# The attention layer's run-time loop, moved from ahead of the last tile to behind the last put-off tile

## The chip, the cores and the metric

The kernel runs on one core of a Trainium2 chip. The metric is the device time of one execution in microseconds (us). The time given is the median of three runs. The profile is that of one further execution, taken by the hardware profiler. The engines are called PE (TensorE), DVE (VectorE), ACT (ScalarE), POOL (GpSimd) and SP (SyncE, which issues most of the transfers).

## The reference, cut to what matters

Four graph layers work on 4096 nodes with 256 features and a 0/1 adjacency matrix. Each layer's result is added to its input and normalized. Layer 1 does two steps of attention with nucleus sparsification, and layer 2 multiplies its neighbour sums by a weight:

```python
# layer 1, for n in range(2):
probs = softmax((Xa @ W1.T @ W2.T) @ (Xa @ W3.T).T)
# of each row keep the largest entries whose sum first reaches 0.9, divide by the kept sum
A  = kept(probs, 0.9)
Xf = R @ Xf                  # R: adjacency plus identity, rows divided by their sums
Xa = A @ Xa
Z  = Z + Xf @ U1[n].T + Xa @ U2[n].T
...
# layer 2: neighbours, then the weight (here taken as adj @ (x @ w2[256:512]) + x @ w2[:256])
support = concatenate((x, adj @ x, nef)) @ weight + bias
```

## The kernel before, in words

The 4096 rows are cut into NT = 32 tiles of 128 rows (P = 128). Layer 0 runs first, then the two steps of layer 1 (`run_step`, n = 0 and 1, called steps 0 and 1), then layers 2 and 3.

**A step of layer 1.** One iteration of the loop over i (L954) works on three tiles at once: it makes the logits of tile i + 2, finds the threshold of tile i + 1, and multiplies tile i. The function `pieces` (L695) writes out the order on PE by hand in NLC = 8 groups g. In step 1 it transposes the kept rows `e` of tile i (`turn`, L716, copied by ACT at L719) and multiplies them with `xa` (L741). The list `ops` says which other functions are called after which group. When a tile is multiplied, `after` (L810) gives two functions that are called in the groups 1 and 2 of the next iteration: `s1` (`mix`: transposes at L177, products with U1 and U2 at L794, the sum on DVE at L796) and `s2` (two layernorms with DVE lines L185 to L196, L819, L820 and the power on POOL at L191; then `put`, which writes the rows into `x2_d` in DRAM). Before tile i is mixed, `fetch` (L767) loads three 128 KB pieces on SP (L777).

**Finding the threshold.** DVE takes 64 candidates of each row (`tops`, L498 and L502), sums them (`pick`) and, in `settle`, sets what is below the threshold to zero: one pass at L628 and four passes over a quarter of the row each at L633. A row for which 64 candidates do not decide is "bad". `flag` (L552) counts the bad rows of a tile on PE (L562, L563) and writes their numbers into a list in DRAM with an indirect DMA (L576). `later["base"]` holds how many there are so far.

**Put-off tiles.** The bad rows are gathered from the list into extra tiles of 128 rows. Step 1 has four of them that are always done (`LATER = (1, 4)`, `put_off`, L869). They are called put-off tiles 0 to 3 here; their buffers and lines in the profile end in `_l`. Each is a generator that is advanced a stage at a time between the groups of `pieces`; `finish` (L936) runs the stages that are left and multiplies the tile. For put-off tiles DVE needs five passes over the whole row (L468) to find the threshold, then L482, L403 and the lines above. Their rows go back with indirect DMAs on POOL (`put`, L762), since they lie anywhere.

**The run-time loop.** If there are more bad rows than four tiles hold, `left_over` (L896) does the rest: two DVE instructions make the trip count (L899, L900), each engine loads it into a register (L901), and a loop (L902) runs over tiles of 128 rows, with a bit-by-bit search in place of the candidates. In the profile it makes no trip: its body has no record. In step 1 it stands at the head of the iteration i = 31, after tile 30's `s1` and `s2` and before tile 31 is multiplied. Its body uses the buffer `es[0]`, the keys `kS` and `xa`.

**Tile 31.** It is multiplied after the loop. So that it does not overwrite what the loop wrote for its own bad rows, `flag` makes a list of targets for tile 31 alone, `to_last` (L575), in which a bad row points to a spare row behind the 4096. `put` then writes tile 31 with an indirect DMA on POOL over `x2_d` (L762). Layer 0 writes tile 31 of `x2_d` once, so that all of it has been written.

**Products with layer 2's weight.** After the last tile, `z_room` (L828) loads the weight into `es[1]`, and 32 calls of `zu_tile` load a tile of `x2_d` (L852, four slots), multiply it (L177, L843), copy the result (L846) and write it to `zu_d` (L853). Sixteen stand beside the products of put-off tile 2, sixteen beside the stages of put-off tile 3. A put-off tile that ends after `z_room` makes its own products: in `s2` (L823) it calls `zu` and writes `zu_d` with an indirect DMA (L762).

**Layer 2** begins with four pieces of the adjacency matrix (L1077, 128 KB each, on SP; cast by ACT at L1079), the loads of `zu_d` into a scratch area (L157) which DVE and ACT split into two halves (L142, L143, L144), and four weights on ACT's queue (L84, L131). Its tiles lie where `kS`, `es` and the other buffers of layer 1 were, and each waits until those under it are free. Then PE multiplies (L167).

**Order.** Tile, the framework, puts the instructions in order when the kernel is compiled: for each engine it takes what is ready by its own estimate of the times, with the order of the program as the priority. Waits between engines are semaphores, set for the region of a buffer that an instruction touches; an indirect write counts as a write to the whole of the tensor it names. A run-time loop is one unit in this order. What depends on nothing in it can be put ahead of it.

Of the kernel before, what the change touches and what calls it, by code (L numbers as in the profile page):

```python
# [48 lines left out]
def gnn_stack(ctx, tc, x, adjt, adjn, w0, b0, w1, w2t, w3t, u1t, u2t, ln_g, ln_b, w2, b2, w3, b3, out):  # L49
# [3 lines left out]
    nc = tc.nc  # L53
    N = x.shape[0]
    NT = N // P
# [22 lines left out]
    def half(bank):  # L78
        turns[bank] ^= 1
        return (mm_bank if bank == "mm" else acc_bank)[:, turns[bank], :]  # L80
# [25 lines left out]
    x2_d = dram.tile([N + P, D], F32, name="x2_d")  # L106
# [16 lines left out]
    def rows(t, it):  # L123
        return t[it * P : (it + 1) * P, :]
# [46 lines left out]
    def transposed(*srcs):  # L171

        n = 2 * len(srcs)
        ps = ps_tr.tile([P, 4, P], F32, tag="tr", name="tr")
        for s, src in enumerate(srcs):
            for c in range(2):
                nc.tensor.transpose(ps[:, 2 * s + c, :], src[:, c * P : (c + 1) * P], ident)  # L177
        t = work.tile([P, 4, P], F32, tag="xt", name="xt")
        nc.scalar.copy(t[:, :n, :], ps[:, :n, :])  # L179
        return t  # L180
# [33 lines left out]
    with tc.tile_pool(name="l0", bufs=1) as l0, tc.tile_pool(name="l0w", bufs=2) as l0w:  # L214
# [18 lines left out]
        x1 = xpool.tile([P, NT, D], F32, tag="X", name="x1")  # L233
# [53 lines left out]
        def l0_end(it, agg):  # L287
            xi = l0w.tile([P, D], F32, tag="x0i", name="x0i")
            nc.scalar.dma_start(xi, rows(x, it))
            xt = transposed(xi, agg)  # L290
            ps = half("mm")
            for c in range(4):
                nc.tensor.matmul(ps, xt[:, c, :], w0_sb[:, c, :], start=(c == 0), stop=(c == 3))
            t = l0w.tile([P, D], F32, tag="t", name="t")
            nc.vector.tensor_add(t, ps, b0_sb)
            nc.vector.scalar_tensor_tensor(t, t, 0.0, xi, op0=ALU.max, op1=ALU.add)
            ln_apply(x1[:, it, :], t, ln_stats(t))

            x1b = l0w.tile([P, D], F32, tag="x1b", name="x1b")
            nc.vector.tensor_add(x1b, x1[:, it, :], lb_sb)  # L300
            nc.sync.dma_start(rows(x1_d, it), x1[:, it, :])
            nc.sync.dma_start(rows(x1b_d, it), x1b)
            if it == NT - 1:

                nc.sync.dma_start(rows(x2_d, it), x1[:, it, :])

        def l0_keys(it):
            make_keys(transposed(x1[:, it, :]), kS[:, it * P : (it + 1) * P])
# [16 lines left out]
    with tc.tile_pool(name="l1", bufs=1, reuse_waits="tile") as l1:  # L325

        cur = {"late": False, "n": 0, "nef_done": False}
# [224 lines left out]
        def flag(st):  # L552


            pb = half("mm")
            later = st.get("later")
            if later is None:
                nc.tensor.matmul(pb[:1, 0:1], st["bad"], ones_col, start=True, stop=True)
                st["nb"] = small("nbad", 1, I32)[:1, :]
                nc.scalar.copy(st["nb"], pb[:1, :1])  # L560
                return
            nc.tensor.matmul(pb[:, 0:1], ones_sq, st["bad"], start=True, stop=True)  # L562
            nc.tensor.matmul(pb[:, 1:2], before, st["bad"], start=True, stop=True)  # L563
            sofar, slot = small("sofar"), small("slot")
            nc.vector.tensor_add(sofar, later["base"], pb[:, 0:1])

            i = st["tile"]
            at, rows_i = slots_of[cur["n"]][:, i : i + 1], ids[:, i : i + 1]
            nc.vector.scalar_tensor_tensor(slot, pb[:, 1:2], later["base"], spare, op0=ALU.add, op1=ALU.subtract)
            nc.vector.scalar_tensor_tensor(at, slot, st["bad"], spare, op0=ALU.mult, op1=ALU.add)  # L570
            later["base"] = sofar
            if i == NT - 1:

                st["to"] = to = small("to_last", 1, I32, 1)
                nc.vector.scalar_tensor_tensor(to, st["bad"], float(P), rows_i, op0=ALU.mult, op1=ALU.add)  # L575
            nc.gpsimd.indirect_dma_start(  # L576
                out=list_d[cur["n"]], out_offset=bass.IndirectOffsetOnAxis(ap=at, axis=0), in_=rows_i, in_offset=None)
# [318 lines left out]
        def left_over(n, e, later):  # L896

            count = work.tile([P, 1], I32, tag="count_l", name="count_l", bufs=1)
            nc.vector.tensor_scalar(count, later["base"], float(P - 1 - LATER[n] * P), 0.0, op0=ALU.add, op1=ALU.max)  # L899
            nc.vector.tensor_scalar(count, count, P.bit_length() - 1, None, op0=ALU.arith_shift_right)  # L900
            v = nc.values_load(count[0:1, 0:1], min_val=0, max_val=NT - LATER[n])  # L901
            with tc.For_i(0, v, 1) as k:  # L902
                cur["late"] = True
                st, xg = take_rows(n, bass.ds(k * P + LATER[n] * P, P), e)
                all_logits(st, query(xg))
                peak(st)
                exp_rows(st)
                st["t"], st["left"], st["base"] = small("t_thr"), small("left"), None
                for _ in settle(st, True):
                    pass  # L910
                pieces(n, st, None, {})
                for f in after(n, st):
                    f()
                cur["late"] = False

        def run_step(n, es):
# [3 lines left out]
            later = {"base": spare0}  # L920
# [33 lines left out]
            for i in range(-2, NT):  # L954
                st = tiles.pop(i, None)
                cd = tiles.get(i + 1)
                nxt = None
                if i + 2 < NT:

                    nxt = {"tile": i + 2, "q": cur["qs"].pop(0), "e": logits_in(es[i % 2]), "later": later, "G": {}}  # L960
                    tiles[i + 2] = nxt
                if i + 1 == NT:
                    for fs in last:
                        for f in fs:
                            f()
                    last = []
                    left_over(n, es[NT % 2], later)
                ops = {}

                def at(g, f, *args):  # L970
                    ops.setdefault(g, []).append(lambda: f(*args))

                for g, fs in zip((1, 2), last):
                    for f in fs:
                        at(g, f)
                if 0 < i + 2 < NT - 1:
                    turned = []
                    g = 1 if n else 6
                    at(g - 1, lambda i, turned: turned.append(transposed(cur["xa"][:, i + 3, :])), i, turned)
                    at(g, lambda turned: cur["qs"].append(query(None, turned[0])), turned)  # L980
                if cd is not None:
                    peak_groups(cd)
                    at(1, exp_rows, cd)
                for job in jobs:
                    at(1, advance, job)
                if cd is not None:
                    rounds = 8 if n else KEPT // 8
                    at(2, tops, cd, rounds)
                    at(2, pick, cd, rounds)
                    at(4, flag, cd)  # L990
                    if n == 0:
                        for k in range(8):
                            at(4 + k // 2, gather, cd, k)
                    else:
                        at(5, lambda cd: [None for _ in settle(cd)], cd)
                for job in jobs:
                    if n and i + 1 == NT:
                        at(4, advance, job)
                    at(6, advance, job)
                if i + 1 == NT and n == 0:  # L1000
                    cur["next"] = load_halves(es[1 - NT % 2], xf_d, nc.sync)
                if i < 0:
                    now = FIRST[n][i + 2]
                else:
                    now = [i + 2] if FIRST[n][1][-1] < i + 2 < NT else []
                pieces(n, st, nxt, ops, now)
                last = [[f] for f in after(n, st)] if st is not None else []
                if i in starts:
                    k = starts[i]
                    if len(jobs) > (i == NT - 2):  # L1010
                        last = finish(jobs.pop(0), last)
                    e = es[NT % 2] if k + 1 == LATER[n] else es[2]
                    jobs.append({"stages": put_off(n, k, e, later)})
                    if i < NT - 2:
                        advance(jobs[-1])
# [22 lines left out]
            for fs in last:  # L1038
                for f in fs:
                    f()  # L1040

        for n in range(STEPS):
            cur["n"] = n
            with tc.tile_pool(name=f"step{n}", bufs=2, reuse_waits="tile") as cur["w"], \
                    tc.tile_pool(name=f"late{n}", bufs=1, reuse_waits="tile") as cur["lw"]:
                es = [cur["w"].tile([P, N + PAD], F32, tag=f"e{k}", name="e", bufs=1) for k in range(2 + n)]
# [152 lines left out]
```

## Time and profile before

| | |
|---|---|
| median of three runs | 3354.87 us (3349.98 to 3359.43) |
| the profiled execution's own time | 3313.77 us |
| its span, first to last instruction | 3312.0 us |
| mean granted PE clock in it | 0.965 |
| PE busy | 3017.6 us (91%) |
| DVE busy | 2393.5 us (72%) |
| ACT busy | 1873.9 us (57%) |
| POOL busy | 782.7 us (24%) |

The profiled execution is 41.1 us shorter than the median of the runs, and 1.8 us of it lie outside the span. Times in the profile count from the start of the span. Step 1 ends with tile 31's work at about 2585 to 2633 us, the two last put-off tiles up to about 2774 us, and layer 2 starts after that. In a row of the timeline the two first numbers are start and length in us; "x8" says that eight instructions were merged; the bracket gives how long the engine stood idle before it and what ended that.

### The profile page before, as it was taken

Reading aid. Unit: us, or ns where it says so; the run is one execution under the profiler, and the core shown is the slowest. Engines: PE = TensorE matmul, PEld = TensorE weight load, DVE = VectorE, ACT = ScalarE, POOL = GpSimd, SP = SyncE. Lnnn points to the kernel's source line nnn. Section 1 sums busy time; section 2 is a strip of 40 time slices with the busy share of each in tenths; the row PEclk is TensorE's granted clock in tenths of the full one; section 3 lists DMA queues with packets and bytes.
Section 4 is the critical chain, followed back from the end, with each engine's and each line's share of the span. In section 5 each row is a group of like instructions: output and inputs, shape, how many; then the busy total and the mean of one; then the engine's idle time right before and its main releaser. Section 6 shows DMA issues by size and latency. Waiting matters only on the chain. (4 is left out here: it accounts for less than half of the span.)

```text
span 3312.0 us, 46373 instructions
## 1 busy us (share of the span) xinstructions
PE 3017.6 (91%) x14600; PEld 2465.7 (74%) x14600; DVE 2393.5 (72%) x7121; ACT 1873.9 (57%) x3162; POOL 782.7 (24%) x916
## 2 busy tenths in 40 slices
PE   6999888999999997879989898989999787999998
PEld 5888667888888885658877777777788545888886
DVE  6888858878777776357988897888799673444444
ACT  3555666777777774455555454545455333666664
POOL 1111146666666665100000001000100001000000
PEclk9999989999999998889999999999999898999999
DMA  9988367787777776140000111011011133333332
GB/s 175 143 134 139 68 105 130 135 138 137 136 137 137 136 137 143 56 134 30 25 23 23 32 38 31 26 32 39 24 38 30 42 131 126 110 109 107 102 108 81
DMA packets 247906, 300.30 MB, mean 91 GB/s; under 512 B 34688, under 2 KB 201536, under 8 KB 247648
## 3 DMA queue, kind: packets, MB, share of 16 engines
q0 software_dynamic: 46624, 105.07, 22.8%
q1 hardware_dynamic: 188800, 180.93, 18.8%
q10 hardware_dynamic: 12224, 11.23, 1.1%
q8 instruction: 118, 1.93, 0.3%
q14 instruction: 140, 1.15, 0.1%
HBM read 331.17 MB, written 66.58 MB: 120 GB/s over the span
## 5 line engine op out<-in xcount | busy, mean ns | idle before, releaser
L656 PE MATMUL acc_r<-xh,adjq 128*128 128x512 f32 x2048 | 617.5, 433 | 22.4 <-ACT adjq L653 17.7
L741 PE MATMUL acc_bank<-xa,at 128*128 128x256 f32 x2304 | 568.8, 388 | 31.0 <-ACT at L719 30.5
L642 POOL DMA_INDIRECT G<-x_d,cols x512 | 499.4, 975 | 302.2 <-PE acc_bank L733 163.0
L167 PE MATMUL acc<-xh,a 128*128 128x512 f32 x2048 | 516.5, 405 | 17.8 <-DVE xh L144 14.0
L741 PEld LDWEIGHTS acc_bank<-xa,at 128*128 128x128 f32 x2304 | 425.3, 194 | 92.1 <-ACT at L719 41.3
L653 ACT CAST adjq<-adj 128x512 fp32r<-128x512 uint8 x512 | 316.0, 619 | 295.1 <-PE acc_r L656 97.8
L656 PEld LDWEIGHTS acc_r<-xh,adjq 128*128 128x128 f32 x2048 | 382.7, 193 | 117.6 <-ACT adjq L653 42.2
L167 PEld LDWEIGHTS acc<-xh,a 128*128 128x128 f32 x2048 | 384.6, 191 | 103.0 <-ACT xh L143 17.0
L403 DVE MAX8 cand<-e 128x8 f32<-128x256 f32 x1024 | 381.1, 414 | 93.1 <-ACT e L385 92.0
L191 POOL TENSOR_TENSOR rstd<-ve,mhalf 128x1 f32<-128x1 f32 x168 | 102.7, 611 | 1378.7 <-DVE ve L189 1338.9
L385 ACT COPY e<-lg 128x512 f32<-128x512 f32 x552 | 318.9, 584 | 176.9 <-PE lg L384 176.0
L384 PE MATMUL lg<-kS,q 128*128 128x512 f32 x1104 | 392.2, 440 | 10.7 <-ACT e L385 10.4
L1079 ACT CAST a<-a 128x1024 fp32r<-128x1024 uint8 x256 | 267.7, 1048 | 150.4 <-PE acc L167 121.7
L733 PE MATMUL acc_bank<-G,dg 128*128 128x256 f32 x1024 | 277.8, 392 | 51.5 <-DMA G<-x_d,cols 40.6
L500 DVE FIND_INDEX8 cols<-top,e 128x8 uint32<-128x4096 f32 x64 | 282.8, 4419 | 0.0
L733 PEld LDWEIGHTS acc_bank<-G,dg 128*128 128x128 f32 x1024 | 194.7, 194 | 100.7 <-DMA G<-x_d,cols 49.0
L719 ACT COPY at<-at_ps 128x512 f32<-128x512 f32 x296 | 173.5, 588 | 113.1 <-PE at_ps L716 111.6
L167 PE MATMUL acc<-yh,a 128*128 128x512 f32 x1024 | 233.7, 390 | 0.0
L252 ACT CAST a<-a 128x1024 fp32r<-128x1024 uint8 x128 | 133.5, 1048 | 157.4 <-PE acc L167 121.3
L167 PEld LDWEIGHTS acc<-yh,a 128*128 128x128 f32 x1024 | 192.2, 188 | 39.6
L384 PEld LDWEIGHTS lg<-kS,q 128*128 128x128 f32 x1104 | 182.9, 192 | 32.5 <-ACT e L385 19.4
L716 PE MATMUL at_ps<-ident,e 128*128 128x128 f32 x1184 | 183.5, 279 | 22.0 <-issue 13.8
(281 smaller groups left out, 4637.2 us busy)
## 6 DMA issues: line engine op xcount, KB each, us to landing
adj<-adj_d SPq DMA_DIRECT2D x256, 128.0 KB
a<-adj_d SPq DMA_DIRECT2D x256, 128.0 KB
a<-in_adjt POOLq DMA_DIRECT2D x64, 256.0 KB
adj_d<-a SPq DMA_DIRECT2D x64, 256.0 KB
adjn<-in_adjn POOLq DMA_DIRECT2D x64, 256.0 KB
x_d<-x SPq DMA_DIRECT2D x65, 128.0 KB
G<-x_d,cols POOLq DMA_INDIRECT x512
xf_d<-xf_new SPq DMA_DIRECT2D x64, 128.0 KB
```

The costliest lines, as they stand in the source:

```text
L167: nc.tensor.matmul(acc, a[:, j, :], halves(jt), start=(jt == 0), stop=(jt == NT - 1))
L384: nc.tensor.matmul(pl[:, :LC], q[k], kS[:, s], start=(k == 0), stop=(k == 1))
L385: nc.scalar.copy(l[:, s], pl[:, :LC])
L403: nc.vector.max(dst[:, 8 * g : 8 * g + 8], src[:, g * GW : (g + 1) * GW])
L500: nc.vector.max_index(st["at"][:, 8 * r : 8 * r + 8], t8, st["e"][:, :N])
L642: nc.gpsimd.indirect_dma_start(out=g, out_offset=None, in_=x1_d, in_offset=bass.IndirectOffsetOnAxis(ap=st["at"][:, k : k + 1], axis=0))
L653: nc.scalar.copy(a, cur["a8"][:, g % 2 * GP : (g % 2 + 1) * GP, :])
L656: nc.tensor.matmul(acc_r, a[:, j, :], xf[:, jt, :], start=(jt == 0), stop=False)
L716: nc.tensor.transpose(ps[:, j, :], e[:, (g * G + j) * P : (g * G + j + 1) * P], ident)
L733: nc.tensor.matmul(acc_a, dg[:, k % 4, :], st["G"][k], start=(k == 0), stop=(k == KEPT - 1))
L741: nc.tensor.matmul(acc_a, ats[g][:, j, :], cur["xa"][:, jt, :], start=(jt == 0), stop=(jt == NT - 1))
L1079: nc.scalar.copy(a, a8)
```

## The change

The loop of step 1 moves from the head of the iteration i = 31 to the very end of `run_step`, behind the last put-off tile. Tile 30's `s1` and `s2`, which were called ahead of the loop, go back to the groups 1 and 2 of tile 31's `pieces`, as for every other tile. Since `z_room` has been called by then, the loop's body now also holds the products with layer 2's weight (L823). Tile 31 no longer needs `to_last` in step 1, so its rows go to `x2_d` with an ordinary DMA on SP (L765) and `fetch` loads as before. Layer 0's early write of tile 31 to `x2_d` goes. Step 0 keeps its loop and its `to_last`.

```diff
@@ layer 0, l0_end
             nc.sync.dma_start(rows(x1b_d, it), x1b)
-            if it == NT - 1:
-
-                nc.sync.dma_start(rows(x2_d, it), x1[:, it, :])
@@ flag
-            if i == NT - 1:
+            if i == NT - 1 and cur["n"] == 0:
 
                 st["to"] = to = small("to_last", 1, I32, 1)
@@ run_step, head of an iteration
-                if i + 1 == NT:
+                if i + 1 == NT and n == 0:
                     for fs in last:
                         for f in fs:
                             f()
                     last = []
                     left_over(n, es[NT % 2], later)
@@ run_step, its end
             for fs in last:
                 for f in fs:
                     f()
+            if n > 0:
+                left_over(n, es[NT % 2], later)
```

## The prediction

> **What bounds the kernel now.** I read the page's first lines, then the timelines of PE, DVE and SP around the loop, the wait tables from 2590 to 2800 us, and last the chain of work from 2560 to 2800 us.
>
> ```profile
> span 3312.0 us, 46373 instructions
> PE 3017.6 (91%) x14600; PEld 2465.7 (74%) x14600; DVE 2393.5 (72%) x7121; ACT 1873.9 (57%) x3162; POOL 782.7 (24%) x916
> ```
>
> PE is the bound over the whole, but the change touches only 2590 to 2800 us, so what counts is why PE stands still there. The loop, PE and then DVE:
>
> ```profile
> 2591.21 3.69 PE L794 MATMUL mm_bank<-u,xt 128*128 128x256 f32 x8 [0.47 <-DVE match L626]
> 2608.71 1.97 PE L716 MATMUL at_ps<-ident,e 128*128 128x128 f32 x8 [13.81 <-issue]
> 2610.50 2.60 PE L741 MATMUL acc_bank<-xa,at 128*128 128x256 f32 x8
> ```
>
> ```profile
> 2596.00 1.28 DVE L633 SCALAR_TENSOR_TENSOR e<-e,t_thr 128x1024 f32<-128x1024 f32 x1
> 2597.20 0.08 DVE L633 DVE_READ_ACCUMULATOR e<-e,t_thr 128x1 f32 x1
> ...
> 2604.64 0.41 DVE L196 TENSOR_SCALAR h<-h,bn,rstd 128x256 f32<-128x256 f32 x1 [0.73 <-POOL rstd L191]
> 2609.63 1.28 DVE L633 SCALAR_TENSOR_TENSOR e<-e,t_thr_l 128x1024 f32<-128x1024 f32 x1 [4.58 <-DMA xf<-xf_d]
> ```
>
> PE stands still for 13.81 us and then starts tile 31. Yet the first quarter of tile 31's `e` is final at 2597.28. The rest of the wait is the loop: every engine reads the trip count, and the loop is left only when tile 30's last layernorm (L196, ends at 2605.05), its DMA and all earlier transfers are done. The loop's line shows how it is passed with no trip:
>
> ```profile
> L902 DVEq EVENT_SEMAPHORE  x13: 21/50/50, 2605.2 to 2609.3; - x13
> L902 SPq EVENT_SEMAPHORE  x13: 17/28/28, 2605.6 to 2607.5; - x13
> L902 POOLq INC_SWDGE_SEM  x1: 1939/1939/1939, 2604.9 to 2604.9; - x1
> ```
>
> A second stop of PE, 50 us later, hangs on tile 31's target list (PE, POOL, then SP's waits):
>
> ```profile
> 2666.29 1.11 PE L177 MATMUL tr<-ident,e 128*128 128x128 f32 x4 [7.17 <-DMA e<-x_d]
> ```
>
> ```profile
> 2661.58 1.02 POOL L762 DMA_INDIRECT x_d<-h,to_last  x1 [0.74 <-DVE lo_l L472]
> ```
>
> ```profile
> SPq L852 <- DMA x_d<-h,to_last: 7.4, 1, 7.4
> ```
>
> The loads of `x2_d` for the products with layer 2's weight wait for an indirect write of tile 31, since it counts as a write to all of `x2_d`. Last, the end of layer 1 in the chain, and SP's and ACT's early work for layer 2:
>
> ```profile
> 2773.80 5.03 DMA zu_d<-e,to_l
> 2778.96 3.49 DMA scratch<-zu_d
> 2782.47 0.70 DVE scratch L142
> 2783.20 1.23 DVE xh L144
> ...
> 2784.57 3.92 PE acc L167 x8
> ```
>
> ```profile
> 2734.67 1.87 SPq L1077 DMA_DIRECT2D a<-adj_d  x4
> ```
>
> Here nothing but this chain runs; the four adjacency pieces were fetched at 2734.67 and cast by 2778.7, under its cover.
>
> **What the Trainium skill says.** "TensorE: Matmul & The Clock Gate", section "What's actually happening": after an idle window of about 3.4 us PE runs at half clock. The trace agrees: the granted clock is 0.67 from 2590 to 2600 us and 0.50 from 2600 to 2610, and L794's eight products took 3.69 us there against 2.00 at 2648. "Advanced Engine Details and Errata", section "Control Flow Timing": a compare-and-branch takes about 108 ns. L902's take 33 to 66 ns on four engines and up to 312 on PE; so the loop costs by its waits, not by its branches. "DMA: Bandwidth & Descriptors", section on the anatomy of one DMA: about 2 us fixed, mostly until the write is confirmed. The indirect write of `zu_d` took longer: 5.03 us from its start, of which 0.96 is issue; I use the trace. "SBUF — State Buffer", section "SBUF: two separate sides": GpSimd and DVE lock a shared port pair against each other. The trace fits: tile 31's power on POOL (L191) took 4.58 us beside a DVE pass of 4.49 (L468), against 0.54 to 0.73 at the loop; this is part of why tile 31's write came as late as 2661.58.
>
> **Part 1: the loop leaves tile 31's path.** PE can start tile 31 at 2597.28 instead of 2608.71, since waits go by region: SP's load over the first columns of the same buffer (L832) started at 2610.28, after the first transposes alone. That is 11.4 us. It assumes that PE still does tile 30's `mix` in the gap (its input is there at 2586.4, and the compiler's order fills idle time with what is ready). Below: if `mix` comes behind tile 31's first groups, 2.4 us go (0.38 + 2.00 at full clock); if the compiler puts put-off tile 2's four L633 passes, which now wait behind the loop, ahead of tile 31's, 4 x 1.21 = 4.8 more. Above: the first transposes and products ran cold, 1.97 + 2.60 against 1.04 + 2.00 at 2632 to 2636, 1.5 us. I take 11.4, from 4.2 to 12.9.
>
> Does it reach the end? From 2666 to 2733 PE has no idle over 0.8 us: it is bound by the 2.3 us of each product tile, and put-off tile 3's `e`, ready on DVE at 2715.5, waits until 2733.48. This slack of 18.0 us is DVE's. DVE starts put-off tile 3's chain behind L633's passes of put-off tile 2, which now follow at about 2601 instead of 2609.63, 8.6 us earlier. So PE may gain 18.0 + 8.6 = 26.6 us before DVE is the bound.
>
> **Part 2: tile 31's write is ordinary.** It now touches tile 31's rows alone, so loads of other tiles need not wait for it. The stop of 7.17 us goes, and with it the cold products behind it (1.11 + 4.83 against 0.60 + 3.70, 1.6 us): 8.8 us at best. But the write moves from POOL's queue to SP's, in which the loads and the stores of the products stand; those behind it wait until tile 31's layernorm is done, which comes late beside DVE's passes. If the first blocked load stands behind it, only the landing is saved, 2664.10 - 2661.58 = 2.5 us. Four slots are loaded ahead, and the slot of the seventh load is free at about 2643, well before, so most loads should be ahead: I take 6.5, from 2.5 to 8.8.
>
> **Part 3: the end of layer 1 pays.** Behind the last write of `zu_d` now stands the loop. First, passing it: SP took 0.91 us from 2606.81 to its first DMA at 2607.72. POOL's INC_SWDGE_SEM (1.94 us here, 0.74 in step 0) lies under the landing, or behind it: 0.9 to 2.8, I take 2.0. POOL has nothing behind it; SP's loads, ACT's casts and PE's first product do wait. Second, the early work for layer 2 is no longer early: the keys `kS`, under the first adjacency pieces, are read in the loop's body, so they can't go ahead of it. The four issues take 1.87 us of SP ahead of the first scratch load. Third, these 0.5 MB and ACT's four weights, 0.64 MB, which moved between 2773 and 2779, now share the transfer engines with the scratch loads. From 2785 to 2790 us these moved 264 GB/s at a share of 0.79; 1.15 MB at that rate is 4.3 us; what other waits in this phase hide of it is open, 0 to 4.3, I take 3.0. Sum 6.9, from 2.8 to 9.0. The four casts of 1.05 us lie beside the scratch load.
>
> **The rest.** Layer 0's DMA was one of 128 KB beside a busy PE: 0. L575 (0.15 us of DVE) falls away in the idle before 2590.78: 0. The body's added products have no record, as there is no trip: 0. If there were one, the body would stand on the path.
>
> **Sum.** -11.4 - 6.5 + 6.9 = -11.0 us, on the profiled execution 3313.77 to 3302.8. The runs' median is 41.1 us higher; the stops are waits and latencies, so I carry the microseconds over: 3354.87 - 11.0, about 3344.
>
> **The rivals.** (a) Forecast, both stops go and the end pays about 7: 3339 to 3349. (b) Given back: the order takes part 1 down to 4.2, part 2 is 2.5 to 6.5, the end costs 9.0, which gives +2.3 to -1.7; from there half-way to (a) at -5.5: 3349 to 3357. For it: the end has no cover at all. Against: PE's stops have a named cause that is removed. (c) Slower: SP's queue. If the compiler sets tile 31's write ahead of the product tiles' stores, SP stands from about 2642, where it is ready to store, to the write's 2661; the four output slots fill, and PE's stop grows from 7.2 to as much as 2661 - 2647 = 14 us, so part 2 costs 7 instead of saving 6.5. With part 1 at 6.6 (L633 ahead) and the end at 9.0, that is +9: 3364. The sign turns where PE's second stop is not at least 9.0 - 6.6 = 2.4 us shorter than its 7.2 of now. Against it: the compiler knows the length of DVE's passes. (d) More: part 1 12.9, part 2 8.8, the end 2.8: -18.9, 3336.
>
> **How the numbers follow.** A difference of 0.3%, 10 us, is about what a measurement of this kernel tells from no change. (a) 0.50, (b) 0.28, (c) 0.12, (d) 0.10. Some 0.30 of (a) and all of (d) lie beyond -10 us: faster 0.40. Of (c) 0.05 lies beyond +10 with the runs' own scatter of some 5 us: slower 0.06. Same 0.54. The range, 3334 to 3361, holds (a), (b) and (d) nearly whole and the milder part of (c).
>
> **What would show it.** Right: PE's first L716 of tile 31 some 2 us after the first L633 of tile 31 ends, no idle on L902 there; no 7 us stop "<-DMA e<-x_d"; PE's idle ahead of the first L167 of layer 2 grows from 11.7 us to about 17 and the first tile of layer 2 starts slower. Wrong: put-off tile 2's L633 between tile 31's, an x_d write on SP with a long wait ahead of L852 or L853, or adjacency pieces issued ahead of the loop, in which case part 3 is near 2.

## The result, and the profile after

| | before | after |
|---|---|---|
| median of 14 runs each | 3352.06 us | 3342.02 us |
| lowest and highest | 3343.31 to 3362.02 | 3333.44 to 3351.03 |
| ratio after/before | | 0.9967, 95% interval 0.9957 to 0.9976 |
| profiled execution, own time | 3313.77 us | 3340.46 us |

The change saves 10.0 us by the medians, 8.0 to 14.4 by the interval. The forecast was 3344 us, 11.0 less than the median that was shown.

The profiled execution of before was 30 us shorter than the shortest of its 14 runs, so the two profiles cannot be laid side by side from their starts. I aligned them at tile 31's maximum on DVE (the L435 `m<-cand`; L432 after the change), because from there DVE, not PE, sets the pace. A second profile of before (first experiment) confirms this point: from it to the end of the kernel the two executions of before take 746.2 and 746.1 us. Lines after the change are those of before less 3 (less 1 in layer 2): L713 was L716, L630 was L633, L899 was L902.

The first two lines of the page after:

```profile
span 3338.8 us, 46384 instructions
PE 3024.1 (91%) x14600; PEld 2462.3 (74%) x14600; DVE 2395.2 (72%) x7120; ACT 1873.3 (56%) x3162; POOL 781.6 (23%) x915
```

The busy times hardly change (PE's grows by 6.5 us of 3017.6); what has moved is waits. Tile 31 in PE's timeline of the changed kernel:

```profile
2629.44 0.58 PE L559 MATMUL mm_bank<-bad,ones_sq 128*128 128x1 f32 x2 [11.11 <-DVE bad L531]
...
2636.94 1.94 PE L713 MATMUL at_ps<-ident,e 128*128 128x128 f32 x8 [6.49 <-DVE e L630]
2638.75 3.38 PE L738 MATMUL acc_bank<-xa,at 128*128 128x256 f32 x8
...
2644.13 0.38 PE L177 MATMUL tr<-ident,xf 128*128 128x128 f32 x2
...
2645.43 1.96 PE L791 MATMUL mm_bank<-u,xt 128*128 128x256 f32 x8
```

The 13.81 us behind the loop are gone: PE now waits for tile 31's own pass on DVE. But that pass is late, and tile 30's `mix` (L177, L791) stands between tile 31's groups, though PE idled for 11.11 and 6.49 us just before. DVE's timeline shows why the pass is late:

```profile
2620.01 1.27 DVE L630 SCALAR_TENSOR_TENSOR e<-e,t_thr_l 128x1024 f32<-128x1024 f32 x1
...
2622.26 1.27 DVE L630 SCALAR_TENSOR_TENSOR e<-e,t_thr_l 128x1024 f32<-128x1024 f32 x1
...
2623.71 1.28 DVE L630 SCALAR_TENSOR_TENSOR e<-e,t_thr_l 128x1024 f32<-128x1024 f32 x1
...
2625.12 1.27 DVE L630 SCALAR_TENSOR_TENSOR e<-e,t_thr_l 128x1024 f32<-128x1024 f32 x1
...
2629.22 0.16 DVE L531 SCALAR_TENSOR_TENSOR bad<-left,bad 128x1 f32<-128x1 f32 x1
...
2635.50 1.28 DVE L630 SCALAR_TENSOR_TENSOR e<-e,t_thr 128x1024 f32<-128x1024 f32 x1
```

The four passes with `t_thr_l` are put-off tile 2's. Before, they stood behind the loop; now they are put in between tile 31's searches for its candidates, ahead of `bad`. At the second stop, PE's timeline has only this, and SP's instructions of the line that writes a tile to `x2_d` (first and last start in the row) are those of tiles 29, 30 and 31:

```profile
2666.93 0.60 PE L177 MATMUL tr<-ident,e 128*128 128x128 f32 x4
```

```profile
L762 SPq DMA_DIRECT2D x_d<-h x3: 319/319/319, 2622.2 to 2692.6; - x3
```

The first transposes for layer 2's weight follow without a wait. Tile 31's write is issued at 2692.61, well behind the first loads. Last, the end of layer 1, in the chain:

```profile
2794.78 3.17 DMA zu_d<-e,to_l
...
2799.03 4.39 DMA w2e_sb<-in_w
...
2803.43 0.37 SPq L157
...
2803.84 5.71 DMA scratch<-zu_d
```

and in the timelines of SP and PE:

```profile
2798.86 1.74 SPq L1076 DMA_DIRECT2D a<-adj_d  x4
2803.43 0.92 SPq L157 DMA_DIRECT2D scratch<-zu_d  x2
```

```profile
2809.46 2.05 PE L167 MATMUL acc<-xh,a 128*128 128x512 f32 x4 [15.58 <-DMA a<-adj_d]
```

The same place in PE's timeline of before:

```profile
2784.57 3.91 PE L167 MATMUL acc<-xh,a 128*128 128x512 f32 x8 [11.68 <-DVE xh L144]
```

PE's idle grew from 11.68 to 15.58 us. SP leaves the loop and issues the adjacency pieces from 2798.86 to 2800.60, but the first scratch load comes only at 2803.43. The chain names a wait that I had not thought of, the load of `w2e_sb` by ACT, and so does the table of SP's waits:

```profile
SPq L157 <- DMA w2e_sb<-in_w: 2.8, 1, 2.8
```

Where the time went, in us from tile 31's maximum on DVE. "Weight" is the first product with layer 2's weight, "put-off 3" the first transposes of put-off tile 3, "last write" the issue of the last indirect write of `zu_d`, "layer 2" its first product, "result" the first transposes of a finished row tile of layer 2:

| kernel | tile 31 on PE | weight | put-off 3 | last write | layer 2 | result | end |
|---|---|---|---|---|---|---|---|
| before | 42.9 | 70.7 | 167.6 | 208.0 | 218.7 | 249.3 | 746.2 |
| after | 35.8 | 66.7 | 154.4 | 193.7 | 208.4 | 240.7 | 737.7 |
| difference | -7.0 | -4.0 | -13.3 | -14.3 | -10.4 | -8.6 | -8.5 |

So part 1 gave 4.0 (at the weight), part 2 another 9.3 (at put-off 3), and of the 14.3 at the last write 5.7 were given back behind it. A single profile places a stage to about 1 us. In the five other profiles of kernels that do the same work up to there (third, fourth, seventh, eighth and tenth experiment) the weight comes 3.7 to 4.7 us earlier than before; and the stretch from put-off 3 to the last write, 40.3 us before and 39.3 after, takes 39.3 in three of the five and 40.4 and 40.6 in the two others. The 8.5 us at the end lie at the lower end of the interval of the runs (8.0 to 14.4); whether an earlier stage adds a little is open.

### The profile page after: what moved, and what is told of

It reads as the page before. It is cut to its first block, busy times and chain, and to the rows that moved or that the text cites. A ratio compares the mean times of both kernels' runs of the same rounds, so it can differ in the third digit from the quotient of the medians.

```text
span 3338.8 us, 46384 instructions
## 1 busy us (share of the span) xinstructions
PE 3024.1 (91%) x14600; PEld 2462.3 (74%) x14600; DVE 2395.2 (72%) x7120; ACT 1873.3 (56%) x3162; POOL 781.6 (23%) x915
## 5 line engine op out<-in xcount | busy, mean ns | idle before, releaser
L167 PE MATMUL acc<-xh,a 128*128 128x512 f32 x2048 | 516.5, 405 | 23.1 <-DMA a<-adj_d 15.6
L716 ACT COPY at<-at_ps 128x512 f32<-128x512 f32 x296 | 173.8, 589 | 102.5 <-PE at_ps L713 100.8
L713 PE MATMUL at_ps<-ident,e 128*128 128x128 f32 x1184 | 183.5, 279 | 14.7 <-DVE e L630 14.6
```

The costliest lines, as they stand in the source:

```text
L167: nc.tensor.matmul(acc, a[:, j, :], halves(jt), start=(jt == 0), stop=(jt == NT - 1))
L713: nc.tensor.transpose(ps[:, j, :], e[:, (g * G + j) * P : (g * G + j + 1) * P], ident)
```

## The experiments

The times from tile 31's maximum that are given below come from one profile each; the ratios come from the runs. The theory after this reading: part 1 was cut by the order on DVE and on PE, part 2 was larger than taken, and part 3 was paid, partly to a wait that the forecast did not know. Rivals: DVE or POOL is the next bound, so that the order on PE does not matter; the end is bound by bytes, not by that wait.

**Before again.** No edit.

> The kernel before, unchanged, for a second profile of it. The profiled execution shown of it was 30 us shorter than any of its 14 timed runs, so its stages can only be laid beside those of the changed kernel after an alignment at the last products of tile 30. Theory A, that execution gained its time earlier than this stage: from the last products of tile 30 (16 merged, 3.62 us) to the first product of layer 2 it takes 203.4 us as in the profile shown, within 1 us; then of the 10.0 us by which the medians differ, 6.9 come from the stage up to the third tile of layer 2 and 3 are not placed. Theory B, the stage itself is longer in an ordinary execution: it takes 3 us more, and the 10.0 us are all in this stage.

Measured: 3353.39 us, span 3351.7. From tile 31's maximum: 42.8, 70.7, 167.7, 208.0, 218.9, 249.6, 746.1 in the table's columns. From the last products of tile 30 to layer 2 it takes 203.6 us, so theory A holds: the profile shown had gained its time earlier. Half of the "3 us that are not placed" came from my first anchor. Tile 30's last product on PE starts 18.54 us after the maximum in before, where the clock granted to PE over the 20 us behind the maximum is 0.91 on average, and 16.85 us after it in the changed kernel, where it is 1.00; DVE's chain does not move. With the anchor on DVE the stage holds 8.5 us of the 10.0.

**Part 2 alone.** On the kernel before:

```diff
-            if i == NT - 1:
+            if i == NT - 1 and cur["n"] == 0:
```

(and without layer 0's early write)

> The kernel before with tile 31 of step 1 written by an ordinary DMA on SP, and without layer 0's early write; the loop stays ahead of tile 31. It leaves out the protection of tile 31's own rows against being overwritten after the loop (the loop makes no trip). By the step of the prediction: -6.5 us against before (2.5 to 8.8). By the two profiles, laid one on the other: -9.3, the 7.17 us stop of PE that ends with the load of x2_d gone and some 2 us of cold products behind it. Rival: DVE is next behind PE's stop, so that put-off tile 3 ends no earlier: 0 to -2.

Measured: ratio 0.9971 (0.9953 to 0.9989), median 3339.16 of 6. Put-off tile 3 starts at 158.4, 9.3 us earlier than before; the last write at 199.1 (-8.9); the end at 739.0 (-7.2). The first transposes for layer 2's weight (at 2670.09) follow without a wait. Part 2 is 9.3 at its place, and the rival falls. Behind the last write 1.7 us of it are lost again, although this kernel's loop stands where it was.

**Parts 1 and 3 without part 2.** On the changed kernel:

```diff
-            if i == NT - 1 and cur["n"] == 0:
+            if i == NT - 1:
```

(and layer 0's early write put back)

> The changed kernel, but with tile 31's target list and indirect write kept in step 1 (and layer 0's early write with it): parts 1 and 3 without part 2. By the steps of the prediction: -11.4 + 6.9 = -4.5 us against before. By the profiles: -2.3 + 5.7 = +3.4 us, since put-off tile 2's last passes stand ahead of tile 31's threshold on DVE, and the 7 us stop is back.

Measured: ratio 0.9993 (0.9980 to 1.0006), no measurable difference. In its PE timeline the stop is back:

```profile
2690.19 1.09 PE L177 MATMUL tr<-ident,e 128*128 128x128 f32 x4 [7.25 <-DMA e<-x_d]
```

Weight at 66.0 (-4.7), put-off 3 at 163.1 (-4.5), end at 745.7 (-0.5). By the profile, moving the loop by itself gains about as much as it costs; the runs (-6.7 to +2.0 us) leave room for the forecast's -4.5, but not for my +3.4.

**Without the loop.** On the changed kernel:

```diff
-            if n > 0:
-                left_over(n, es[NT % 2], later)
```

> The changed kernel without step 1's loop at all; it leaves out the loop, which makes no trip with these inputs. What it gains over the changed kernel is what part 3 costs. By the step of the prediction 6.9 us, so -17 us against before; by the profiles 5.7, so -15.7. The adjacency pieces and the weights are again fetched ahead of the last write of zu_d and the first product of layer 2 starts some 11 us after that write, not 15. Rival: the end of layer 1 was bound by the landing of that write alone, and no more than 1 us is gained (-11).

Measured: ratio 0.9960 (0.9944 to 0.9975). Up to the last write (193.9) it is the changed kernel; then layer 2 starts at 204.9, the result is at 236.5 and the end at 733.2, 4.4 us before the changed kernel's 737.7. Part 3 costs 4.4 by the profiles, so the rival (under 1 us) falls; the runs cannot tell this kernel from the changed one (0.9957 to 0.9976).

**Tile 30's mix first.** On the changed kernel:

```diff
-                if i + 1 == NT and n == 0:
+                if i + 1 == NT:
                     for fs in last:
                         for f in fs:
                             f()
                     last = []
+                if i + 1 == NT and n == 0:
                     left_over(n, es[NT % 2], later)
```

> The changed kernel, but tile 30's mix and layernorms called ahead of tile 31's groups, as before the change. In the changed kernel the mix (0.38 + 1.96 us of PE) stands between tile 31's groups, although PE idles 11.1 us ahead of them. Theory A, the order of PE costs part 1 this much: measured from the last product of tile 30, put-off tile 3's first logits come 3.0 us earlier than in the changed kernel (40.0 to 37.0), and so does the end of the stage. Theory B, PE waits for the next thing from DVE or POOL anyway: less than 0.5 us at the first product with layer 2's weight.

Its PE timeline:

```profile
2631.28 3.75 PE L791 MATMUL mm_bank<-u,xt 128*128 128x256 f32 x8 [0.47 <-DVE match L623]
2637.50 1.11 PE L713 MATMUL at_ps<-ident,e 128*128 128x128 f32 x8 [2.46 <-DVE e L630]
```

The mix now fills the wait (at half clock, 3.75 us), and the weight comes at 64.3, 2.45 earlier than in the changed kernel: theory A at this place, with 2.45 for 3.0 (1.8 to 2.8 against all six profiles with the changed kernel's order). At the end only 0.2 is left (737.5). 1.6 of it went between put-off 3 and the last write, a stretch that takes 39.3 us in five profiles and 40.3 to 40.9 in the others. Kernels that are identical up to there fall on both sides (39.3 in the changed kernel, 40.4 in the eighth experiment), so the execution alone can make this difference. But all three kernels with the mix first (fifth, ninth and eleventh experiment) are on the longer side, so that the edit has a part in it is not ruled out. One profile cannot say what this edit is worth at the end.

**Tile 31's passes first on DVE.** In `settle`, ahead of the passes:

```diff
+            if cur.get("first") is not None and cur["late"] and not loop:
+                nc.vector.scalar_tensor_tensor(t, cur.pop("first"), 0.0, t, op0=ALU.mult, op1=ALU.add)
...
             whole(st, kept)
+            if cur["n"] == 1 and st.get("tile") == NT - 1:
+                cur["first"] = st["sc"]
```

> The changed kernel, but the four L630 passes of put-off tile 2 made to depend on the end of tile 31's own passes (one instruction on DVE of some 0.2 us that adds nought to their threshold), so that tile 31's chain is first on DVE. Theory A, those passes ahead of it are what took part 1 down: tile 31's count of bad rows comes 5.6 us after the last product of tile 30 as in the kernel before, not 11.7, tile 31's first transposes at about 13, not 19.0, and all that follows up to the last write of zu_d 6 us earlier; 6 us less than the changed kernel in all, about -16 us against before. Theory B, DVE becomes the bound behind it, since put-off tile 2's passes and put-off tile 3's chain come later: less than 2 us at the end. By the prediction's own reckoning (first transposes 1.4 us behind the first pass) part 1 is then near its 11.4.

Measured: ratio 0.9958 (0.9946 to 0.9970), median 3338.70 of 20. Its PE timeline and DVE's (L632 is the pass here):

```profile
2625.77 0.59 PE L559 MATMUL mm_bank<-bad,ones_sq 128*128 128x1 f32 x2 [6.66 <-DVE bad L531]
...
2633.26 1.94 PE L717 MATMUL at_ps<-ident,e 128*128 128x128 f32 x8 [6.49 <-DVE e L632]
```

```profile
2631.82 1.28 DVE L632 SCALAR_TENSOR_TENSOR e<-e,t_thr 128x1024 f32<-128x1024 f32 x1
```

`bad` is back where it was before (23.7 us after the maximum, 28.1 in the changed kernel), tile 31 starts on PE at 31.4, the weight at 62.8 and the last write at 189.8: 4.5, 3.9 and 3.9 us earlier than in the changed kernel. Theory A, with 4 in place of 6 us, since the 6 came from the anchor on PE. Theory B falls at the last write. At the end 2.8 us are left (734.9), and the runs cannot tell this kernel from the changed one (0.9957 to 0.9976).

**Layer 2's weights behind the scratch loads.** On the changed kernel:

```diff
-        w2e_sb = load_bcast(l23, w2[2 * D, :], "w2e_sb")
+        w2e_sb = load_bcast(l23, w2[2 * D, :], "w2e_sb", nc.sync)
...
```

(the same for `b2_sb`, `w3_sb` and `b3_sb`; the loading functions take the queue as an argument)

> The changed kernel, but layer 2's four weights loaded on SP behind the first two scratch loads, not on ACT ahead of them. In the changed kernel the first scratch load starts 8.65 us after the last write of zu_d; SP had passed the loop and issued the four adjacency pieces after 6.0, and then waited until the load of w2e_sb had landed, with which it shares a semaphore (eight are handed round among all the loads). Theory A, this shared semaphore costs 2.6 us: the first scratch load starts at 6.0, the first product of layer 2 comes 2.6 us earlier or a little more. Theory B, the prediction's third term (the transfer engines are shared, 3.0): the scratch load starts at 8.6 or lands sooner by 3. Theory C, none of it: the casts of the adjacency pieces end last and the first product stays at 14.7.

Measured: ratio 0.9963 (0.9953 to 0.9974), end at 735.1, 2.6 us earlier than in the changed kernel, which the runs cannot tell. The scratch load starts 5.9 us after the last write (8.65 in the changed kernel), and layer 2 12.2 us after it (14.7). By its start this fits theory A; but the weights' bytes are out of the way too, so it does not separate A from B. The next one was made to do that.

**The weights where they were, another semaphore.** On the changed kernel:

```diff
+        nc.scalar.dma_start(zu_d[N : N + 1, :D], b2[None, :])
         ahead = [piece(0, c) for c in range(NJP)]
```

> The changed kernel with one more load of 1 KB on ACT ahead of layer 2's weights (into a row behind the 4096 of zu_d, which nothing reads). It only turns the order of the eight semaphores on by one: the first scratch load now shares one with this small load, the second with the first adjacency piece; the weights move at the same time as before. Theory A, the shared semaphore was the wait: the first scratch load starts 6.0 to 6.5 us after the last write of zu_d, not 8.65, and the first product of layer 2 some 2 us earlier. Theory B, the bytes of the weights were what cost: the first product stays where it is, since the scratch load takes longer to land.

The timelines of its SP, DVE and PE; the last write was issued at 2797.10:

```profile
2803.70 0.92 SPq L157 DMA_DIRECT2D scratch<-zu_d  x2
```

```profile
2810.60 0.69 DVE L142 TENSOR_SCALAR scratch<-scratch 128x1024 int32<-128x1024 int32 x1 [18.86 <-DMA a<-adj_d]
```

```profile
2812.70 3.79 PE L167 MATMUL acc<-xh,a 128*128 128x512 f32 x8 [16.50 <-DMA a<-adj_d]
```

The scratch load starts 6.6 us after the write, as theory A wants, and is of use only 6.9 us later (2810.60 - 2803.70); in the changed kernel, where it waits, 3.93 (2807.36 - 2803.43). (The bracket of L142 is an inference of the view: by the trace's semaphore records the scratch load itself was confirmed at 2810.58.) Layer 2 starts at 15.6, not at 12.7. Theory A falls, though the chain names that wait: an earlier start gained nothing while the weights moved. The edit was not as clean as expected, though. The small load put the next three weights 0.7 to 0.9 us further behind the last write, and the fourth was issued only at 2811.33. The 0.9 us by which layer 2 came later may be that, and how much the bytes alone cost is not shown here.

**Three edits together** (the mix first, tile 31's passes first, the weights behind).

> The changed kernel with three edits together: tile 30's mix ahead of tile 31's groups, tile 31's passes ahead of put-off tile 2's on DVE, and layer 2's weights behind the first two scratch loads. If the three costs add up (2.4, 3.9 and 3.0 us in the profiles of the single edits), the stretch from tile 31's maximum on DVE to the end takes 737.7 - 9.3 = 728.4 us, against 746.2 before: about -18 us against before. Rival: with the first two DVE is the bound in front of put-off tile 3, and some 4 us are given back: -14.

Measured: median 3330.68 of 6, ratio to before 0.9939 (0.9917 to 0.9961), by the two ratios 9.4 us under the changed kernel. Tile 31 starts at 31.6, the weight comes at 60.5 (6.2 us earlier than in the changed kernel; 2.45 + 3.9 = 6.35), the end at 730.5, not 728.4. Up to put-off 3 (148.2, 6.2 us earlier) the first two costs add up, and the rival falls there. 1.0 of the missing 2.1 is the stretch between put-off 3 and the last write, which took 40.3 us here. The stage is then 15.7 us shorter than before, between the theory's 18 and the rival's 14, and the runs (13 to 28) do not decide. With the last experiment's kernel it is the best version found: its interval lies below 1 altogether, and overlaps only a little with that of the changed kernel (0.9957 to 0.9976).

**Neither loop nor weights ahead.** On the changed kernel, the edits of the fourth and seventh experiments together.

> The changed kernel without step 1's loop (it is left out; it makes no trip) and with layer 2's weights behind the first two scratch loads. The last write of zu_d took 5.0 us to land wherever there was no loop behind it, and 3.2 with the loop. Theory A, in the kernels without the loop the four weights (0.64 MB) move at the same time as this write and slow it: here they come later, it lands in about 3.2 us, the first scratch load starts 3.3 us after the write's start, and the first product of layer 2 some 9 us after it (11.1 without the loop and with the weights ahead, 12.2 with the loop and the weights behind). Theory B, the weights have nothing to do with it: 5.0 as before, the first product at 10.8 to 11.1, and passing the loop and the four issues cost 1.2 us.

The chain of the kernel without the loop (weights ahead), then of this one:

```profile
2793.84 5.02 DMA zu_d<-e,to_l
2798.99 3.79 DMA scratch<-zu_d
```

```profile
2799.47 2.70 DMA zu_d<-e,to_l
2802.30 3.61 DMA scratch<-zu_d
```

The same write lands in 2.70 us when the weights do not move beside it, and in 5.02 when they do. From the last write to layer 2's first product, in us:

| | weights ahead | weights behind |
|---|---|---|
| no loop | 11.1 | 8.6 |
| loop | 14.7 | 12.2 |

Theory A. Up to layer 2's first product the loop costs 3.6 us with the weights in either place, the weights 2.5 with and without the loop. Further on this no longer holds: up to the result of the first row tile the loop costs 4.4 with the weights ahead but 2.0 with them behind, and the weights 3.2 with the loop but 0.8 without it. What limits that stretch was not tested.

**The adjacency pieces on ACT's queue**, on the kernel with three edits: `queue.dma_start(a8, ...)` with `nc.scalar` for the first four.

> As the kernel with the three edits, and the four adjacency pieces issued on ACT's queue, so that SP has the first scratch load as its first work behind the loop. By the prediction's term for the issues, 1.87 us: the first scratch load starts 4.1 us after the last write of zu_d instead of 5.9, and the first product of layer 2 comes 1.9 us sooner. Rival: the pieces move beside the scratch load, and the first piece and its cast, not the scratch load, end last: 0 to -0.5.

Measured: median 3330.72 of 6, ratio to before 0.9940 (0.9919 to 0.9962); no difference from the kernel with three edits can be told. The scratch load starts at 4.1 us as the term says, but the first product comes at 14.4 (12.5 with the pieces on SP), while the first tile then runs faster: the result is at 231.3 against 233.1, the end at 728.6 against 730.5. At the first product neither expectation holds, since it comes 1.9 us later. The rival had the right kind of reason: the pieces land late beside the scratch load, and ACT, which casts them first, is done with its half of the scratch load only at 2802.33, just ahead of PE's first product at 2802.39. At the end the profile agrees with the term; the runs cannot tell 1.9 us.

## Why the prediction was right or wrong

**The sum** came out (11.0 forecast, 10.0 by the medians, 8.5 in the stage), and so did the likeliest case: both stops gone, and the end paying. That the sum is so close is in part luck. Part 1 was taken 7.4 too large, part 2 2.8 too small and the cost of part 3 2.5 too large, so that errors of 7.4 and 5.3 nearly cancelled. Part 1 ended at the lower edge of its range (4.0 against 4.2 to 12.9) and part 2 above its upper one (9.3 against 2.5 to 8.8). What rival (b) says of part 1, that the order takes it down to 4.2, is what happened; only part 2, which came out whole, kept the result away from (b).

**Part 1, taken 11.4, measured 4.0.** The prediction named what would cut it: 4.8 if put-off tile 2's passes go ahead of tile 31's, 2.4 if `mix` comes behind tile 31's first groups. It took neither; both happened. The runs put 4.5 on tile 31's start (23.7 to 28.1 for `bad`), 3.9 of it at the weight, and 2.45 on the mix. The failed step is "it assumes that PE still does tile 30's `mix` in the gap" and the matching assumption on DVE. The loop had held both in place: it stood behind the mix, and put-off tile 2's passes stood behind it. With the loop gone the passes came to stand in DVE's short idle stretches between tile 31's searches (0.4 to 0.5 us each before), and they take 1.27 us each. That the compiler's own estimate of the times led it to this is argued, not shown. With the order put right by hand PE started tile 31 at 31.4 us, just where the prediction had set it (2597.28 less 2565.85 is 31.4). At the weight the kernel with three edits gains 10.2 of the 11.4. The rest is mostly PE's cold start: tile 31's first eight products took 3.66 us there, 2.60 before, and 1.89 when warm. As "TensorE: Matmul & The Clock Gate" of the Trainium skill has it in "What's actually happening", idle time costs PE its clock. The traces agree: behind 11.11 and 6.49 us of idle the granted clock is 0.50 from 2630 to 2640 us in the changed kernel, and in the kernel with three edits it is 0.67 and 0.65 from 2620 to 2640. So the 1.5 us of warm clock that the term allowed for as an upside were not there to be had.

**That it reaches the end** was right: put-off tile 3 moved with tile 31 in every run, and DVE's last pass for it is done at 143.6 us in the changed kernel, 10.8 before PE takes it up.

**Part 2, taken 6.5, measured 9.3.** The mechanism was right: the stop went, and the loads that PE needed first stood ahead of tile 31's write on SP, as argued. The term was mis-sized by the discount from 8.8 for a blocked load, which did not occur; the last 0.5 are not placed. The slower case, tile 31's write ahead of the stores, had nothing of it in the profile: it was issued 25 us after the first products.

**Part 3, taken 6.9, measured 4.4 by leaving the loop out.** With the weights behind, the loop's 3.66 us up to layer 2's first product can be read off two chains. One is that of the tenth experiment above (no loop), the other that of the seventh (loop):

```profile
2796.03 3.20 DMA zu_d<-e,to_l
...
2801.92 4.21 DMA scratch<-zu_d
```

The last write lands 0.5 later with the loop (3.20 against 2.70). SP then needs 0.9 to its next issue (2799.23 to 2800.13), against 0.1 without the loop (2802.17 to 2802.30), so passing it costs 0.8; POOL's INC_SWDGE_SEM, 2.18 us in the changed kernel, lay under the landing. The four issues take 1.8, and the scratch load takes 0.6 longer beside the pieces (4.21 against 3.61). With the weights ahead the sum is the same 3.6, but made up otherwise: with the loop the write lands 1.85 sooner (3.17 against 5.02), and SP waits 2.8 for `w2e_sb`. The forecast had 2.0 for passing, 1.87 for the issues and 3.0 for "now share the transfer engines". The issues were right and passing was too large; the failed step is the sharing. The pieces cost 0.6. The weights do cost 2.5, but this is not new: in the kernel before they moved beside the last write of `zu_d` and kept it from landing for 2.3 us (5.02 against 2.70). The prediction says itself that the weights moved between 2773 and 2779, and yet that nothing but the chain ran there; I had read the 5.03 us as the cost of an indirect write. "DMA: Bandwidth & Descriptors" of the skill says in "Issuing engines are not separate DMA queues" that transfers of all queues run on the same 16 engines and interleave; the trace agrees with 2.3 us for 0.64 MB beside one write. So the cost only changed its place, and at layer 2's first product the change lost 3.9, near the loop's 3.6.

Behind that point another 1.8 went by the result. From the last write to the result it is 41.3 us before, 47.0 after, and 42.6 both without the loop and in the second experiment, where the loop stands where it was. So by either comparison 4.4 of the 5.7 are the loop's, and where the other 1.3 come from stays open.

**What the prediction said would show it.** PE's first transposes came not 2 us but 0.2 us behind the end of the first pass; there was no idle on the loop; no stop on `x2_d`; PE's idle ahead of layer 2 was 15.6, not 17; the first tile of layer 2 was slower by the 1.8 just named. The sign given for being wrong, put-off tile 2's passes, was there, ahead of tile 31's and not between them.

## What to carry to other kernels

A barrier also holds an order in place: when it is moved, ask what stood behind it, and whether it may now go ahead of the critical chain. A gap on the critical engine may be filled with the wrong work; a dependence that costs one small instruction put it right here and gave back 4 us at the last write. Before a transfer is costed as "now shared", look whether something on the old path was already sharing with it. And a sum that comes out does not show that its terms did.

## What the runs showed of the hardware

- The same indirect write of 128 rows of `zu_d` was confirmed 2.70 us after its start with little else moving, in 3.2 with the loop behind it, and in 5.0 beside 0.64 MB of loads.
- In the semaphore records of the changed kernel the loads of SP and ACT around the end of layer 1 use eight semaphores in turn, so that a load can wait for an unrelated one. The chain then shows this wait (2.8 us on SP); starting the load without it, while the other transfers still moved, brought nothing (in use 6.9 us after its start instead of 3.93, and layer 2 0.9 us later).
- In one stage, two executions whose total times differ by 40 us agree within 0.1 us (746.2 and 746.1), if they are aligned at an instruction of the engine that sets the pace there. An anchor on PE moved by 1.7 us with the clock granted to PE (0.91 or 1.00 over 20 us).
